# Normalised rows interleaved by eight tiles and fetched back in runs of 1 KB; weights of sorted rows loaded in five pieces

## The chip, the cores and the metric

The kernel runs on one core of a Trainium2 chip. The time is device microseconds of one execution. The engines are TensorE (PE, its weight loads PEld), VectorE (DVE), ScalarE (ACT), GpSimd (POOL) and SyncE (SP, which here only issues DMAs).

## What is computed

The input is `x` of shape (4, 32, 128, 128), float32: four images. Two layers follow each other.

```python
# layer 0, per image: xs is x cut in 2x2 patches, 128 channels x 4096 places
energy = einsum('bci,bcj->bij', q, q);  d = sqrt(diagonal(energy))
attn   = softmax(energy / (d_i * d_j))                # 4096 x 4096
x      = gamma * einsum('bcj,bij->bci', q, attn) + xs # back to an image
# layer 1, on tokens t of 128 numbers (4096 per image)
t = t + attn1(ln(t))   # linear attention, no softmax: ln(t) enters through K^T V, a gram of ln(t)
t = t + ffn(ln(t))     # 8 experts, each token takes the 2 with the largest router weights
```

## The kernel before

**Order of the work.** The four images go one after the other through layer 0 (`attend`), which is nearly all of TensorE's work: blocks of 512 x 512 energies (L671, out `pe`), their exponential on ScalarE (L674, `pr`), the product with the values (L559, `po`). The energies are symmetric, so a block is also used in its transposed place: VectorE turns it in groups of 32 x 32 (L482, tile `F`), one DMA stores it to DRAM (L592, `blocks<-F`), six fetch it back with the groups changed over (L607, `F<-blocks`; for diagonal blocks L616 and `F<-below`), and some fifty units of work later TensorE uses it (L495 and L515, `pg`).

The order of the instructions on PE, DVE, ACT and SP is written out when the program is built. Everything else is a generator of small steps, and a step is put in between the blocks of layer 0 when its turn comes. All of the DMAs named here, unless another queue is given, are issued by SP in that order, so that one that waits holds up those behind it.

**Layer 1 of images 0 to 2** runs while the next image is in layer 0. For each group `kc` of eight tiles (0 to 3; a tile has 128 tokens), `close_rows` divides the sums of layer 0, adds them to the tokens `T`, takes mean and variance of each token (L746 to L754 close them: `bs` holds six numbers per tile, and L748 reads one of the six for each of eight tiles) and normalises the rows on ScalarE: `normalise` (L758, L760), one activation per tile, into `xn[:, k, :D]`, a buffer of 32 tiles with 132 numbers each (128 and four for later). `gram_rows` (L778, L789) then adds up the products of each tile with itself on TensorE, in two groups of four tiles: the tile is both weights and moving operand. In the profile each float32 matmul has two records of matmul and two of weight load. Last, the eight tiles go to DRAM (L878, `rows<-xn`).

When all four groups are done, `matrix` (L887) makes one matrix of the gram and the weights. `attention_rows(u)`, again for eight tiles each, needs the rows transposed. `fetch_blocks` (L998) reads them back from DRAM with four DMAs (L1002, `blocks<-rows`), so that block (a, q) of 32 x 32 comes to place (q, a):

```python
blocks[ts(q, S)].rearrange("i k (a c) -> i k a c", c=S),          # S = 32
keep["rows", u][:, :, ts(q, S)].rearrange("(a i) k c -> i k a c", i=S),
```

VectorE then turns each 32 x 32 block with two transposes of 128 x 512 (L1014), the tokens are attended (L919), statistics taken again and the normalised tokens written to `xn` a second time.

**Sorted rows.** Half an image at a time (`sorted_experts(h)`), GpSimd scatters each token's row, with its expert's weight in column 128, to DRAM `xs[h]`, sorted by expert in 39 tiles (L1129). The second half is turned on TensorE. The first half (`turned_by_vector`, L1249) is turned on VectorE: `load_blocks` (L1211, L1215, four DMAs for four tiles) at every fourth step, `turn` (L1221) eight steps later, `four_products` (L1243) eleven steps later, and three steps further the result is multiplied by the tokens' weights (L1227, `factor`) and stored. `factor` is read ahead of the first `load_blocks`, for all 39 tiles in one DMA (L1252): elements of four bytes, 4992 of them.

**The last image** has no layer 0 beside its layer 1. Its rows never go through DRAM (`alone` is true; `transpose_rows` on TensorE does the turning), and its end is `last_parts`.

Of the kernel before, what the change touches and what calls it, by code (L numbers as in the profile page):

```python
# [12 lines left out]
F32 = mybir.dt.float32  # L13
BF16 = mybir.dt.bfloat16
U32 = mybir.dt.uint32
AF = mybir.ActivationFunctionType
# [6 lines left out]
def kernel(  # L23
# [43 lines left out]
    nc = tc.nc  # L67
    P = 128
# [8 lines left out]
    S = 32  # L77
    NH, KQ, D = wk.shape
# [10 lines left out]
    work = ctx.enter_context(tc.tile_pool(name="work", bufs=2))  # L89
    stat = ctx.enter_context(tc.tile_pool(name="stat", bufs=2))  # L90
    dram = ctx.enter_context(tc.tile_pool(name="dram", bufs=2, space=bass.MemoryType.DRAM))
# [626 lines left out]
    def layer1(b, st):  # L718
# [36 lines left out]
            if nm == "f":  # L755
                pinned(nc.gpsimd.tensor_scalar(nbo[:, rows], nb, 1.0, None, ALU.add))

        def normalise(rows, rs, nb):  # L758
            for k in rows:
                nc.scalar.activation(xn[:, k, :D], T[:, k, :], AF.Identity, scale=rs[:, k, :], bias=nb[:, k, :])  # L760

        def transpose_rows(g):
            pt, done = hold(f"ptx_{b}_{g}", partial(keep_rows, g))
# [14 lines left out]
        def gram_rows(rows):  # L778


            def add(p):
                if 0 in rows:
                    nc.vector.tensor_copy(gram, p[:, :D])
                else:
                    nc.vector.tensor_tensor(gram, gram, p[:, :D], ALU.add)

            p, done = hold(f"pgram_{b}_{rows[0]}", add)
            for k in rows:
                nc.tensor.matmul(p[:, :D], xn[:, k, :D], xn[:, k, :D], start=(k == rows[0]), stop=(k == rows[-1]))  # L789
            return done  # L790

        def close_rows(kc):


            def missing():
                return len(st["o"]) < 2 * kc + 2 or any(
                    st["got"][c] < NCH - c - (alone and c == NCH - 1) for c in (2 * kc, 2 * kc + 1)
                )

            late_rows = alone and kc >= 2  # L800
            last_rows = alone and kc == 3

            while "exps" not in st if last_rows else missing():
                yield from idle(1)
            while b > 0 and kc == 0 and not states[b - 1].get("sorted"):
                yield from idle(1)
            den, rd = (stat.tile([P, 2 * NJ], F32, tag=nm, name=f"{nm}_{b}_{kc}") for nm in ("den", "rd"))
            nc.vector.tensor_reduce(den, st["sums"][:, ts(kc, 2 * NJ), :], AX.X, ALU.add)
            nc.vector.reciprocal(rd, den)
            wide = work.tile([P, NJ, 2, 64], F32, tag="grp", name=f"rdx_{b}_{kc}", bufs=2)  # L810
            for s in range(2):
                one = rd[:, ts(s, NJ)][:, :, None]
                nc.vector.tensor_scalar(wide[:, :, s], one.to_broadcast([P, NJ, 64]), gam, None, ALU.mult)
            df = work.tile([P, 8, HW2, 2], F32, tag="df", name=f"df_{b}_{kc}", bufs=1)

            def divide(pb):
                for s in range(2):
                    own = slice(s * 64, s * 64 + 64)
                    o = st["o"][2 * kc + s]
                    for r2 in range(2):  # L820
                        rows = slice(r2 * 64, r2 * 64 + 64)
                        nc.vector.tensor_tensor(
                            df[own].rearrange("p (a k) (h t) r -> p r a (k h) t", a=4, h=2)[:, r2],
                            o[rows].rearrange("p (a j t) -> p a j t", a=4, t=S),
                            pb[own].rearrange("p (j a t) -> p a j t", a=4, t=S),
                            ALU.mult,
                        )

            yield
            if not last_rows:  # L830
                yield
                yield
            pb, done = hold(f"pbd_{b}_{kc}", divide)
            for j in range(NJ):
                nc.tensor.transpose(pb[:, ts(j, P)], wide[:, j].rearrange("p s c -> p (s c)"), ident)
            yield
            while missing():
                yield from idle(1)
            done()
            if not late_rows:  # L840
                yield
                yield
            tk = T[:, ts(kc, 8), :]
            nc.vector.tensor_tensor(tk, tk, df.rearrange("p k w r -> p k (w r)"), ALU.add)
            bs, stats = batch_stats("a", 8 * kc, 8)
            for j in range(8):
                stats[j]()
                if j == 3:
                    yield
                    yield  # L850
            close_stats("a", 8 * kc, 8, bs)
            yield from idle(1 if late_rows else 3)
            k = 8 * kc
            normalise(range(k, k + 4), rsa, nba)
            if late_rows:
                for j in range(k + 4, k + 8):
                    nc.vector.tensor_scalar(
                        xn[:, j, :D], T[:, j, :], rsa[:, j, :], nba[:, j, :], ALU.mult, ALU.add
                    )
            yield  # L860
            if last_rows:
                keep_running(36)
                done = gram_rows([k + j // 2 + 4 * (j % 2) for j in range(8)])
                yield
                done()
                return
            done = gram_rows(range(k, k + 4))
            yield
            done()
            if not late_rows:  # L870
                normalise(range(k + 4, k + 8), rsa, nba)
            yield
            done = gram_rows(range(k + 4, k + 8))
            yield
            done()
            if not alone:
                rows = dram.tile([P, 8, D], F32, tag="rows", name=f"rows_{b}_{kc}", bufs=4)
                nc.sync.dma_start(rows, xn[:, ts(kc, 8), :D])  # L878
                keep["rows", kc] = rows
            if alone and kc < 3:  # L880
                for g in (2 * kc, 2 * kc + 1):
                    yield
                    done = transpose_rows(g)
                    yield
                    done()
# [111 lines left out]

        def fetch_blocks(u):  # L998

            keep["blocks", u] = blocks = work.tile([P, 8, D], F32, tag="wide", name=f"blocks_{b}_{u}")  # L1000
            for q in range(4):
                nc.sync.dma_start(  # L1002
                    blocks[ts(q, S)].rearrange("i k (a c) -> i k a c", c=S),
                    keep["rows", u][:, :, ts(q, S)].rearrange("(a i) k c -> i k a c", i=S),
                )

        def attention_rows(u):
# [3 lines left out]
            yield  # L1011
            for g in (2 * u, 2 * u + 1):
                keep[g] = work.tile([P, CH], F32, tag="grp", name=f"xnT_{b}_{g}", bufs=2)
                nc.vector.transpose(keep[g], keep["blocks", u][:, ts(g % 2, 4), :].rearrange("p k d -> p (k d)"))  # L1014
                yield
            yield
            la = stat.tile([P, 8, 2 * E], F32, tag="la", name=f"la_{b}_{u}")
# [32 lines left out]
        def sorted_experts(h):  # L1050
# [156 lines left out]
            def read(inst):  # L1207
                wait_for(inst.ins, xs_made[h], "a tile holds tokens of any row")
                xs_read[h].append(inst.ins)

            def load_blocks(g, n):  # L1211
                rows = xs[h][4 * g * P : (4 * g + n) * P, :D].rearrange("(m i) w -> i m w", i=S)
                for q in range(4):
                    read(
                        nc.sync.dma_start(  # L1215
                            parts[g % 2][ts(q, S), : n * D].rearrange("i (m c) -> i m c", c=S), rows[:, :, ts(q, S)]
                        )
                    )
# [1 line left out]
            def turn(g, n):  # L1220
                nc.vector.transpose(parts[2 + g % 2][:, : n * D], parts[g % 2][:, : n * D])  # L1221

            def four_products(factor, g, n):

                def leave(p):
                    result = keep["results"].rearrange("p g j c -> p (g j) c")[:, ts(g % 2, 4)]
# [19 lines left out]
                    )  # L1246
                return done

            def turned_by_vector():  # L1249

                factor = stat.tile([P, NT, 1], F32, tag="factor", name=f"factor_{b}_{h}", bufs=1)
                read(nc.sync.dma_start(factor, xs[h].rearrange("(t p) w -> p t w", p=P)[:, :, D : D + 1]))  # L1252
                leaves = {}
                for at in range(4 * len(quads) + 10):
                    for first_at, act in (
                        (8, turn), (0, load_blocks), (11, partial(four_products, factor)), (13, lambda g, n: leaves.pop(g)()),
                    ):
                        if at >= first_at and (at - first_at) % 4 == 0 and (at - first_at) // 4 < len(quads):
                            g, n = quads[(at - first_at) // 4]
                            made = act(g, n)  # L1260
                            if first_at == 11:
                                leaves[g] = made
                    yield
# [380 lines left out]
```

## Time and profile before

| | |
|---|---|
| time before, median of 3 runs | 1620.63 us (1615.23 to 1624.31) |
| profiled execution, its own time | 1636.16 us |
| its span, granted TensorE clock | 1634.4 us, 0.994 |
| PE idle in the span (1634.4 - 1592.9) | 41.5 us |
| DMA queue of SP (q1) | 339776 packets, 308.23 MB, 63.6% of 16 engines |
| DMA packets in all | 374359, of them 159968 under 512 bytes |
| `normalise`, first time (L760, rsa) | 120 activations of 483 ns |
| `gram_rows` on PE (L789) | 256 records, mean 279 ns; 34.7 us busy |
| VectorE's turn of fetched rows (L1014) | 24 transposes, mean 692 ns |
| fetch of rows (L1002) | 48 DMAs of 128 KB |
| `factor` (L1252) | 3 DMAs of 19.5 KB |

A record of a matmul is longer than its share of TensorE's time, since matmuls are pipelined; the spacing of records in the chain tells the share. Idle time of an engine that is not the bottleneck costs nothing by itself. A wait for several things is put down to the one that came last. The trace also has a record of every DMA packet, with its size and the time that it took.

### The profile page before, as it was taken

The page shows a single profiled execution, that of the slowest core. Times are in us where ns is not written, and L with a number is a line of the kernel's source. Part 1 is how long each engine was busy: PE and PEld are TensorE (multiplying, and loading weights), DVE is VectorE, ACT ScalarE, POOL GpSimd, SP SyncE. Part 2 cuts the span into 40 slices and gives each one's busy share as a digit, 9 for nine tenths or more (in the row PEclk, how much of TensorE's full clock was granted, in tenths as well). Part 3 has the DMA queues.
Part 4 walks back from the last instruction along what each step waited for, and adds up shares of the span by engine and source line. Part 5 has one row for each costly group of instructions (what it writes and reads, how often), then busy time and mean ns, then how long its engine had stood idle before and what let it go on. Part 6 is the DMA issues. An engine that isn't in the chain of part 4 may idle for free.

```text
span 1634.4 us, 20871 instructions
## 1 busy us (share of the span) xinstructions
PE 1592.9 (97%) x5019; PEld 830.1 (51%) x5019; DVE 940.0 (58%) x2369; ACT 877.2 (54%) x2779; POOL 596.2 (36%) x567
## 2 busy tenths in 40 slices
PE   8999999999999999999999999999999999998987
PEld 5444544455554454555554445555555455554633
DVE  5443343477686454469478445449568454444786
ACT  4555445466475544556565544556556444544386
POOL 1000000010025541546555542446556641545166
PEclk9999999999999999999999999999999999999999
DMA  5554756676769698998999699998899898884001
GB/s 169 191 204 163 222 184 230 221 237 210 183 211 283 187 240 253 286 254 227 204 250 279 218 231 282 248 276 221 219 234 278 266 238 252 230 272 126 10 14 39
DMA packets 374359, 349.07 MB, mean 214 GB/s; under 512 B 159968, under 2 KB 300768, under 8 KB 359904
## 3 DMA queue, kind: packets, MB, share of 16 engines
q1 hardware_dynamic: 339776, 308.23, 63.6%
q0 software_dynamic: 26624, 25.58, 7.7%
q10 hardware_dynamic: 7840, 13.93, 2.9%
q8 instruction: 42, 0.69, 0.2%
q14 instruction: 77, 0.63, 0.1%
HBM read 170.57 MB, written 182.32 MB: 216 GB/s over the span
## 4 chain that ended last, share of the span: by engine, by line
PE 89%; DVE 3%; DMA 3%; SPq 2%; ACT 1%; issue 1%; another core or an unknown queue 1%; POOL 0%; ACTq 0%; DVEq 0%
PE po L559 26%; PE pe L671 26%; PE pg L495 22%; PE py L1434 3%; PE pg L515 2%; PE pys L1193 2%; PE pgram L789 2%; PE pat L919 1%; PE pys L1243 1%; SPq L607 1%; PE pys L1200 1%; DMA F<-blocks 1%; SPq L1215 1%; DMA ys<-results 0%
## 5 line engine op out<-in xcount | busy, mean ns | idle before, releaser
L674 ACT ACTIVATE pr<-pe 128x512 f32<-128x512 f32 (+1 forms) x576 | 322.5, 560 | 609.4 <-PE pe L671 509.8
L559 PE MATMUL po<-pr,qT 128*128 128x512 f32 (+3 forms) x1152 | 548.3, 558 | 0.2 <-ACT o L564 0.2
L671 PE MATMUL pe<-qn,qn 128*128 128x512 f32 x896 | 458.6, 594 | 3.5 <-ACT pr L674 2.1
L495 PE MATMUL pg<-F,qT 128*128 128x512 f32 x880 | 451.8, 595 | 8.1 <-DMA F<-blocks 5.4
L482 DVE STREAM_TRANSPOSE F<-pr 128x512 f32<-128x512 f32 x440 | 305.1, 699 | 149.2 <-ACT pr L674 128.5
L559 PEld LDWEIGHTS po<-pr,qT 128*128 128x128 f32 x1152 | 216.4, 190 | 240.4 <-issue 224.1
L500 ACT ACTIVATE junk<-F 128x512 bf16<-128x512 f32 x440 | 273.0, 620 | 5.7 <-DMA F<-blocks 4.9
L1308 POOL DMA_INDIRECT acc<-ys,place x128 | 203.2, 1587 | 192.3 <-ACT pr L674 120.3
L495 PEld LDWEIGHTS pg<-F,qT 128*128 128x128 f32 x880 | 166.8, 191 | 203.8 <-issue 179.0
L1129 POOL DMA_INDIRECT xs<-xn,place x192 | 187.1, 975 | 183.4 <-ACT pr L674 111.3
L671 PEld LDWEIGHTS pe<-qn,qn 128*128 128x128 f32 x896 | 157.7, 191 | 130.1 <-issue 119.6
L504 DVE TENSOR_TENSOR o<-o,pg 128x512 f32<-128x512 f32 x110 | 75.0, 682 | 210.9 <-PE pg L495 181.0
L164 POOL TENSOR_TENSOR norm<-ss,neg_half 128x8 f32<-128x8 f32 (+1 forms) x17 | 27.0, 1586 | 311.9 <-DVE ss L296 304.4
L674 ACT ACTIVATION_READ_ACCUMULATOR pr<-pe 128x1 f32 x576 | 111.9, 194 | 0.0
L1308 POOL DMA_INDIRECT yb<-ys,place x64 | 61.2, 956 | 88.0 <-ACT pr L674 47.3
L671 PE MATMUL pe<-qn 128*128 128x512 f32 (+3 forms) x256 | 90.2, 435 | 0.7 <-ACT qn L365 0.7
L500 ACT ACTIVATION_READ_ACCUMULATOR junk<-F 128x1 f32 x440 | 84.4, 192 | 0.0
L1175 DVE TENSOR_TENSOR results<-pys,xn 128x256 f32<-128x256 f32 (+1 forms) x60 | 25.0, 416 | 82.9 <-ACT xn L1169 54.5
L164 POOL TENSOR_TENSOR rsa<-dm_a,neg_half 128x8 f32<-128x8 f32 x16 | 28.4, 1775 | 113.0 <-DVE sv_a L752 112.9
L1434 PE MATMUL py<-ew_sb,xn 128*128 128x512 f32 x128 | 61.5, 622 | 5.1 <-ACT tmp L1390 3.9
L671 PEld LDWEIGHTS pe<-qn 128*128 128x128 f32 x256 | 45.1, 191 | 38.1 <-issue 33.7
L164 POOL TENSOR_TENSOR rsf<-dm_f,neg_half 128x8 f32<-128x8 f32 (+1 forms) x15 | 26.3, 1751 | 103.6 <-DVE sv_f L752 103.6
(226 smaller groups left out, 1506.1 us busy)
## 6 DMA issues: line engine op xcount, KB each, us to landing
blocks<-F SPq DMA_DIRECT2D x110, 1024.0 KB
F<-blocks SPq DMA_DIRECT2D x220, 192.0 KB
F<-blocks SPq DMA_DIRECT2D x220, 128.0 KB
F<-blocks SPq DMA_DIRECT2D x220, 64.0 KB
below<-F SPq DMA_DIRECT2D x31, 384.0 KB
T<-in_x_dram SPq DMA_DIRECT2D x64, 128.0 KB
out_dram<-acc SPq DMA_DIRECT2D x128, 64.0 KB
xa<-in_x_dram SPq DMA_DIRECT2D x62, 128.0 KB
```

Source lines behind the costliest of these rows:

```text
L164: pinned(nc.gpsimd.tensor_tensor(dst, src, neg_half.to_broadcast(list(src.shape)), ALU.pow))
L482: f()
L495: nc.tensor.matmul(pg.rearrange("p (a f) -> p a f", a=4), st["qT"][i][:, ib, :], G[:, :, ib], start=(ib == 0), stop=(ib == NJ - 1),)
L500: nc.scalar.activation(junk, G[:, :, ib], AF.Copy, accum_out=st["sums"][:, NJ * i + ib, jc : jc + 1])
L504: nc.vector.tensor_tensor(st["o"][jc], st["o"][jc], pg, ALU.add)
L515: nc.tensor.matmul(out[:, :, : ib * S], st["qT"][i][:, ib, :], rows, start=(ib == 3), stop=(ib == 1))
L559: nc.tensor.matmul(row["po"][:, lo:hi], qT[blk // NJ][:, blk % NJ, :], w, start=start, stop=(row["left"] == 0))
L671: nc.tensor.matmul(pe[:, c0:], qn[jc][:, ts(j, P)], qn[i][:, c0:], start=True, stop=True)
L674: nc.scalar.activation(pr[:, c0:], pe[:, c0:], AF.Exp, accum_out=sums[:, t, i : i + 1]).ins
L1129: inst = nc.gpsimd.indirect_dma_start(xs[h], offset(place[:, i, k : k + 1]), xn[:, k, :], None)
L1308: inst = nc.gpsimd.indirect_dma_start(to, None, ys, offset(place[:, i, k : k + 1]), compute_op=op)
L1434: nc.tensor.matmul(bank, xn[:, k, :D], ew_sb[:, 4 * h : 4 * h + 4, :], start=True, stop=True)
```

## The change

For images 0 to 2 the eight tiles of a group are written to `xn` so that the eight values of one feature lie next to each other: element (feature d, tile k) is at 8 d + k. One tile's features are then 32 bytes apart, for ScalarE's write and for both operands of the gram. The rows' copy in DRAM has the same order, so that a block of 32 features by eight tiles is one run of 1024 bytes, for the store and the fetch, and VectorE's turn reads elements that are 32 bytes apart. The last image keeps its rows.

The second edit moves the read of `factor` into `load_blocks`, which fetches eight tiles' weights ahead of every second group of four tiles: five DMAs for 39 tiles.

```diff
-        def normalise(rows, rs, nb):
+        def normalise(rows, rs, nb, to=None):
             for k in rows:
-                nc.scalar.activation(xn[:, k, :D], T[:, k, :], AF.Identity, scale=rs[:, k, :], bias=nb[:, k, :])
+                row = xn[:, k, :D] if to is None else side_by_side(to)[:, :, k - 8 * to]
+                nc.scalar.activation(row, T[:, k, :], AF.Identity, scale=rs[:, k, :], bias=nb[:, k, :])
+
+        def side_by_side(kc):
+
+            rows = xn[:, ts(kc, 8), :].rearrange("p k w -> p (k w)")[:, : 8 * D]
+            return rows.rearrange("p (d k) -> p d k", k=8)
...
-                nc.tensor.matmul(p[:, :D], xn[:, k, :D], xn[:, k, :D], start=(k == rows[0]), stop=(k == rows[-1]))
+                row = xn[:, k, :D] if alone else side_by_side(k // 8)[:, :, k % 8]
+                nc.tensor.matmul(p[:, :D], row, row, start=(k == rows[0]), stop=(k == rows[-1]))
...
-            normalise(range(k, k + 4), rsa, nba)
+            place_of = None if alone else kc
+            normalise(range(k, k + 4), rsa, nba, place_of)
...
-                normalise(range(k + 4, k + 8), rsa, nba)
+                normalise(range(k + 4, k + 8), rsa, nba, place_of)
...
-                rows = dram.tile([P, 8, D], F32, tag="rows", name=f"rows_{b}_{kc}", bufs=4)
-                nc.sync.dma_start(rows, xn[:, ts(kc, 8), :D])
+                rows = dram.tile([P, 4, 8 * S], F32, tag="rows", name=f"rows_{b}_{kc}", bufs=4)
+                nc.sync.dma_start(rows, side_by_side(kc).rearrange("p (c s) k -> p c (s k)", s=S))
...
-            keep["blocks", u] = blocks = work.tile([P, 8, D], F32, tag="wide", name=f"blocks_{b}_{u}")
+            keep["blocks", u] = blocks = work.tile([P, 4, S, 8], F32, tag="wide", name=f"blocks_{b}_{u}")
             for q in range(4):
                 nc.sync.dma_start(
-                    blocks[ts(q, S)].rearrange("i k (a c) -> i k a c", c=S),
-                    keep["rows", u][:, :, ts(q, S)].rearrange("(a i) k c -> i k a c", i=S),
+                    blocks[ts(q, S)].rearrange("i a s k -> i a (s k)"),
+                    keep["rows", u][:, q].rearrange("(a i) f -> i a f", i=S),
                 )
...
-                nc.vector.transpose(keep[g], keep["blocks", u][:, ts(g % 2, 4), :].rearrange("p k d -> p (k d)"))
+                nc.vector.transpose(
+                    keep[g].rearrange("p (k a s) -> p k a s", k=4, a=4),
+                    keep["blocks", u][:, :, :, ts(g % 2, 4)].rearrange("p a s k -> p k a s"),
+                )
...
             def load_blocks(g, n):
+                if g % 2 == 0:
+                    tiles = slice(4 * g, min(4 * g + 8, NT))
+                    read(
+                        nc.sync.dma_start(
+                            factor[:, tiles], xs[h].rearrange("(t p) w -> p t w", p=P)[:, tiles, D : D + 1]
+                        )
+                    )
...
+            if h == 0:
+                factor = stat.tile([P, NT, 1], F32, tag="factor", name=f"factor_{b}_{h}", bufs=1)
+
             def turned_by_vector():
 
-                factor = stat.tile([P, NT, 1], F32, tag="factor", name=f"factor_{b}_{h}", bufs=1)
-                read(nc.sync.dma_start(factor, xs[h].rearrange("(t p) w -> p t w", p=P)[:, :, D : D + 1]))
```

More of the change, by code (lines that the diff above doesn't have):

```diff
@@ L1221, in turn, with four_products @@
                 nc.vector.transpose(parts[2 + g % 2][:, : n * D], parts[g % 2][:, : n * D])
-            def four_products(factor, g, n):
+            def four_products(g, n):
                 def leave(p):
@@ L1255, in turned_by_vector @@
                     for first_at, act in (
-                        (8, turn), (0, load_blocks), (11, partial(four_products, factor)), (13, lambda g, n: leaves.pop(g)()),
+                        (8, turn), (0, load_blocks), (11, four_products), (13, lambda g, n: leaves.pop(g)()),
                     ):
```

## Prediction

> **What bounds the kernel now.** I read the page's busy row and chain first, then the windows of 40 us for the stages, then the waits of TensorE, then the chain and the SP queue around the two longest waits, then the lines by form for prices.
>
> ```profile
> PE 1592.9 (97%) x5019; PEld 830.1 (51%) x5019; DVE 940.0 (58%) x2369; ACT 877.2 (54%) x2779; POOL 596.2 (36%) x567
> PE 89%; DVE 3%; DMA 3%; SPq 2%; ACT 1%; issue 1%; another core or an unknown queue 1%; POOL 0%; ACTq 0%; DVEq 0%
> ```
>
> TensorE is busy for 97% of the span and is 89% of the chain; DMA and the SP queue together are 5%. So time can be won only where TensorE stands idle, and whatever TensorE has to do more is paid in full. The windows say where it is idle (time, length, then PE, PEld, DVE, ACT, POOL busy, clock, DMA share, GB/s):
>
> ```profile
> 800.00:840.00 40.00, 37.20 (x131) 20.86 (x130) 25.88 (x88) 22.21 (x70) 21.20 (x17) 1.00 0.96 218
> 840.00:880.00 40.00, 40.00 (x119) 20.12 (x118) 37.02 (x140) 25.72 (x81) 23.54 (x22) 1.00 0.91 273
> 1200.00:1240.00 40.00, 37.75 (x125) 20.22 (x124) 32.34 (x127) 26.71 (x79) 24.31 (x22) 1.00 0.93 252
> ```
>
> From 40 to 1480 us the idle of all windows adds to 15.2 us; the other 26 us are the first 40 us and the end after 1480, which the change doesn't touch (the last image keeps its rows as they were). Of the 15.2, windows 800 and 1200 hold 2.80 and 2.25. These are the stages in which images 1 and 2 fetch their normalised rows. The list of TensorE's waits names them, with everything else that is DMA or comes from the sorted rows:
>
> ```profile
> PE pg L495 <- DMA F<-blocks: 5.4, 3, 2.8
> PE pg L495 <- DVE F L482: 2.7, 3, 1.2
> PE pys L1243 <- DVE xn L1221: 0.6, 1, 0.6
> ```
>
> The SP queue before the wait of 2.8 us (start, time, line, count):
>
> ```profile
> 811.69 5.76 SPq L1002 DMA_DIRECT2D blocks<-rows  x4
> 817.56 0.71 SPq L592 DMA_DIRECT2D blocks<-F  x1
> 818.40 0.35 SPq L1032 DMA_DIRECT2D t<-T  x1
> 818.79 5.59 SPq L1002 DMA_DIRECT2D blocks<-rows  x4
> 829.42 2.68 SPq L607 DMA_DIRECT2D F<-blocks  x6
> ```
>
> The store of F at 817.56 sits between two fetches. Its way back at 829.42 waits for it to land, 11 us; in other places the same pair is 5 us apart (832.20 to 837.23, 963.63 to 968.29). The matmul at 835.01 waits for that way back. The chain names acc<-t as the releaser; a wait is put down to what came last, and L607 needs the store of F, so I take the store.
>
> **The change, part by part.** *Fetch (L1002).* 48 DMAs of 128 KB in pieces of 128 bytes are 49152 packets, 31% of the page's 159968 under 512 B; afterwards 48 x 128 = 6144 of 1 KB. In the trace's packet records one of 128 B takes 14.3 ns on the mean, 512 B 35.4, 2048 B 114.5; between the last two, 1 KB is some 62 ns. On 16 engines that is 44 us before and 24 after: 20 us of DMA time less, in stages where the DMA share is 0.8 to 1.1. SP's issue of four was 2.95 to 6.08 us; F<-blocks, with few packets, takes 2.67 for six, so 1.8 for four. The store of F at 817.56 goes out up to 4 us earlier and lands about 5 us after its issue: its way back starts near 823 at the latest, 6 us before 829.42. The wait of 2.79 goes. Image 2 has the same pattern (store at 1198.52, way back at 1211.37, 12.9 us), and its 2.25 goes. What is late next there: nothing, TensorE has no other wait from 825 to 840 or from 1205 to 1220. **-5.0 us.**
>
> *Store of rows (L878).* Same 12 DMAs, same bytes, but whole runs of 4 KB per partition where there were eight of 512 B. 12288 packets become 1536 or more; hidden, a little less load. Nothing.
>
> *Weights of sorted rows (L1252).* One DMA of 4992 four-byte elements becomes five of at most 1024, the same packets. Before, the first L1215 behind it stood 4.49 us in the SP queue (952.34), on the chain to the matmul that waited 0.63. After, 1024 elements stand ahead of it: about 0.9 us. **-0.6 us.** Each later piece puts about 0.9 us in front of every second load of four, and behind SP's L1215 wait the stores and ways back of F. VectorE's turn of a load comes eight half-steps later and already waits (DVE xn L1221 <- DMA xn<-xs: 37.3 us in 16 times), TensorE felt 0.6 of it; with 12 such pieces at most 12 x 0.9 = 11 us of VectorE waiting, below 1 us of it on TensorE by the same share. Four more DMAs for each of three halves, on SP alone; POOL's queue is not passed.
>
> *VectorE's turn (L1014).* 24 transposes of 692 ns now read with 32 bytes between elements. No transpose of before does; L315 reads at 8 bytes, 413 ns for 256 columns, on the line through 280 (128) and 564 (384). Lower end 0; upper end half speed, 512 x 1.07 = 0.55 us each, 13 us in all. Eight per image; VectorE is 37.0 of 40 us busy in window 840, so cover is thin there: 4.4 us for an image would leave 1 to 2 us on TensorE. *ScalarE (L760).* 96 activations of 483 ns write with 32 bytes between elements; 0 to 0.12 us each (half speed), 11.5 in all, on an engine that waits 510 us for L671. Covered: the grams' own wait for it is 0.5 us today. The rows of an octet now lie between each other: if waits are drawn by the range of bytes and not by the elements, the second four normalisations wait for the first gram (and with them the exponentials queued on ScalarE). That gram is issued half a step earlier and lasts 0.9 us; ScalarE waits for TensorE anyway, so 0, at most 12 x 0.9 = 11 us. I count 1 us for all of these.
>
> *Gram (L789).* This decides. Both operands, weights and moving rows, are now read with 32 bytes between elements, in 96 of 128 products, so 192 of these 256 records:
>
> ```profile
> L789 PE MATMUL pgram<-xn 128*128 128x128 f32 x256 | 34.7, 279 | 0.5 <-ACT xn L760 0.5
> L789 PEld LDWEIGHTS pgram<-xn 128*128 128x128 f32 x256 | 33.3, 191 | 11.8 <-issue 6.7 <-ACT xn L760 3.0 <-ACT pr L674 0.5
> ...
> L750 DVE TENSOR_TENSOR dm_a<-dm_a,sv_a 128x8 f32<-128x8 f32 x16 | 2.7, 167 | 0.5
> L748 DVE TENSOR_TENSOR dm_a<-bs_a 128x8 f32<-128x8 f32 x16 | 2.7, 166 | 0.0
> ```
>
> The chain, by time, has the products of four rows, two records each:
>
> ```profile
> 748.59 0.89 PE pgram L789 x8
> ```
>
> Eight records fill 0.89 us of the chain: 111 ns each, all on the path, no cover. No matmul of before reads elements apart. The nearest row is VectorE's: L748 reads two operands whose elements lie 24 bytes apart and takes 166 ns, L750 with close ones 167. Sixteen elements take 175 (L746), about 1 ns an element, so half speed would show as 8 ns; it doesn't. The Trainium skill speaks against the change: "SBUF — State Buffer", section "Door 1: The DMA port swizzle" (its note on cachelines), says that SBUF has lines of 16 bytes, that two hits per line are needed for full bandwidth, and that fp32 may be four elements apart for free; here it is eight, one hit per line. By the rule with a doubled time (my estimate; the page gives no factor) the grams cost 192 x 111 ns = 21.3 us; by the row, 0. I take 0, nearest to the row, but the row is another engine at about 1 ns an element where TensorE takes 0.83 (107 ns for 128 columns more, L559's 593 against 486), has eight elements, and has no weights read beside it. Both ends stay in the range.
>
> Sum against the profiled execution (1636.16 us, span 1634.4): -5.0 - 0.6 + 1 + 0.6 for the later pieces = -4.0. That execution is 15.5 us above the median; the waits were seen in it alone, and I apply the difference in us: 1620.6 - 4.0 = 1616.6, -0.25%. Changes within 0.5% (8.1 us) are about what a measurement of this kernel can't tell from none.
>
> **Rivals.** (1) *Likeliest, 0.50*: strided reads cost TensorE nothing or up to 15 ns a record (3 us): 1614 to 1620, within 0.5%. (2) *Slower: the gram reads at half speed.* Place: L789 in the stages 338 to 403, 748 to 785, 1122 to 1166; price 21.3 - 4.0 = +17, 1638. It turns to slower by over 0.5% at (8.1 + 4.0) / 192 = 63 ns a record, 1.6 times. For it: the rule, two strided streams at once, no cover. Against: VectorE's row. 0.32, with a tail over 1642 (0.06 of it) if weights and rows take turns at the port: another 21 us, 1659. (3) *In between*: a record at 1.04 ns an element, VectorE's pace: +27 ns, 5.1 us, or ScalarE and VectorE give back what the fetch gains: 1620 to 1628. For it: DVE 37.0 of 40. 0.12, a sixth of it over 0.5%. (4) *Hidden anyway*: the store of F is late for another reason (other traffic, the DMA share is 0.96), and the waits stay: 1620 to 1621, counted in case 3's lower half. (5) *Faster by over 0.5%*: 8.1 of the 15.2 us of idle would have to go, though 5.0 of it (windows 1280, 1400 and 1440, 2.12 + 1.52 + 1.39) lies where no rows are fetched: under 1612.5, 0.06.
>
> Faster 0.06, slower 0.32 + 0.02 = 0.34, same 0.60. The range takes the likeliest case and half speed, from 1612 to 1642, and leaves out some 0.06 on either side. The likeliest case's own range is 1614 to 1620.
>
> **What would show it.** Right: blocks<-rows issues in about 1.8 us for four, packets under 512 B fall by about 49000; no wait of pg L495 for F<-blocks above 0.5 us in the fetch stages; the first L1215 behind a factor load under 1.5 us; pgram still 0.89 us for eight, its LDWEIGHTS still 191. Wrong: pgram at 1.8 us for eight or LDWEIGHTS near 300 ns (rival 2); L1014 near 1.2 us or L760 near 0.6 with new TensorE waits for them (rival 3); the F<-blocks wait of 2 to 3 us still there (rival 4). A cost of the grams that shows only in the spacing of records, not in their length, would also make it wrong.

## The result, and the profile after

The changed kernel takes 1638.64 us (median of 6 runs, 1637.50 to 1642.01) against 1620.69 us before: ratio 1.0122, 95% interval 1.0106 to 1.0138. It is slower by 18 us between the medians (17 to 22 by the interval), where the likeliest case of the prediction was 4 us faster. The time lies within the range, at the place of rival 2 (1638).

The profiled executions can't be set against each other as wholes. That of before lay 15.5 us above its median: TensorE's granted clock fell to half in five spells (mean 0.994), where that of after has two (0.998), and some waits near the end are in it alone. So its span is only 2.4 us shorter than the one of after (1636.8). What follows is read line by line.

The page after, busy time and the chain by engine:

```profile
PE 1609.5 (98%) x5019; PEld 852.1 (52%) x5019; DVE 951.4 (58%) x2369; ACT 879.8 (54%) x2779; POOL 596.3 (36%) x567
...
PE 91%; DVE 3%; DMA 2%; SPq 2%; ACT 1%; issue 1%; POOL 0%; ACTq 0%; DVEq 0%
```

TensorE has as many instructions as before and is busy 16.6 us longer, its weight loads 22 us. The lines by form say where (the gram is L796 now, VectorE's turn L1022, ScalarE's normalisation L761):

```profile
L796 PE MATMUL pgram<-xn 128*128 128x128 f32 x256 | 58.3, 383 | 1.5 <-ACT xnT L781 0.9 <-ACT xn L761 0.6
L796 PEld LDWEIGHTS pgram<-xn 128*128 128x128 f32 x256 | 57.3, 296 | 10.0 <-issue 3.1 <-ACT xn L761 2.2 <-ACT xnT L781 1.2
L761 ACT ACTIVATE xn<-T,nba,rsa 128x128 f32<-128x128 f32 x120 | 51.7, 572 | 5.1 <-POOL nba L754 5.1
L1022 DVE STREAM_TRANSPOSE xnT<-blocks 128x512 f32<-128x512 f32 x24 | 25.8, 1085 | 9.8 <-PE pat L927 9.8
...
L750 DVE TENSOR_TENSOR dm_a<-dm_a,sv_a 128x8 f32<-128x8 f32 x16 | 2.7, 167 | 0.5
L748 DVE TENSOR_TENSOR dm_a<-bs_a 128x8 f32<-128x8 f32 x16 | 2.7, 166 | 0.0
```

The gram's matmuls are busy 58.3 us where they were 34.7, the turn went from 692 to 1085 ns, the activation from 483 to a mean of 572. The last two rows, on which the prediction had rested its choice, are as they were. In the chain, by time, the products of four rows:

```profile
339.50 1.89 PE pgram L796 x8
...
747.01 1.89 PE pgram L796 x8
...
1134.38 1.89 PE pgram L796 x8
```

That is 236 ns a record where it was 111. There are 24 such groups in images 0 to 2: 24 x (1.89 - 0.89) = 24.0 us, all on TensorE.

The windows that had 2.80 and 2.25 us of idle, and the thin cover of VectorE between them:

```profile
800.00:840.00 40.00, 40.00 (x138) 22.21 (x137) 23.34 (x60) 19.13 (x61) 20.89 (x15) 1.00 0.79 205
840.00:880.00 40.00, 40.00 (x126) 20.73 (x125) 36.22 (x136) 29.33 (x90) 25.57 (x22) 1.00 0.84 241
...
1200.00:1240.00 40.00, 39.91 (x148) 22.97 (x148) 29.88 (x90) 22.72 (x71) 22.38 (x18) 1.00 0.81 222
```

TensorE has no gap there any more (0.09 us is left), and the DMA share fell from 0.96 and 0.93 to 0.79 and 0.81. The packets under 512 bytes went from 159968 to 111008, 48960 fewer. Of TensorE's waits for the things named before, two are left:

```profile
PE pg L495 <- DMA F<-blocks: 2.8, 4, 0.9
...
PE pg L495 <- DVE F L482: 0.9, 1, 0.9
```

And the SP queue where the store of F stood between two fetches (the fetch is L1010):

```profile
822.60 2.40 SPq L1010 DMA_DIRECT2D blocks<-rows  x4
825.23 0.34 SPq L592 DMA_DIRECT2D blocks<-F  x1
831.17 0.34 SPq L1043 DMA_DIRECT2D t<-T  x1
831.57 2.23 SPq L1010 DMA_DIRECT2D blocks<-rows  x4
833.90 10.71 SPq L607 DMA_DIRECT2D F<-blocks  x6
```

The four DMAs of a fetch issue in 1.7 to 3.5 us where they took 3.0 to 6.1, and the way back of F begins 8.7 us after the store instead of 11.9. But only two of its six DMAs go then; the other four, in the same row, leave at 842.69:

```profile
842.69 1.92 SPq L607 DMA_DIRECT2D F<-blocks  x4
```

So the gaps that the change was built to close are closed, though not as the prediction had it (taken up below), and 24.0 us are lost elsewhere.

### The profile page after: what moved, and what is told of

The parts are those of the page before. It is cut to its first block, busy times and chain, and to the rows that moved or that the text cites. A ratio compares the mean times of both kernels' runs of the same rounds, so it can differ in the third digit from the quotient of the medians.

```text
span 1636.8 us, 20878 instructions
## 1 busy us (share of the span) xinstructions
PE 1609.5 (98%) x5019; PEld 852.1 (52%) x5019; DVE 951.4 (58%) x2369; ACT 879.8 (54%) x2779; POOL 596.3 (36%) x567
## 2 busy tenths in 40 slices
DMA packets 320792, 349.08 MB, mean 213 GB/s; under 512 B 111008, under 2 KB 245664, under 8 KB 306336
## 4 chain that ended last, share of the span: by engine, by line
PE 91%; DVE 3%; DMA 2%; SPq 2%; ACT 1%; issue 1%; POOL 0%; ACTq 0%; DVEq 0%
PE po L559 26%; PE pe L671 26%; PE pg L495 22%; PE pgram L796 3%; PE py L1453 3%; PE pg L515 2%; PE pat L927 2%; PE pys L1204 2%; PE pys L1261 1%; DMA F<-blocks 1%; SPq L1233 1%; PE pys L1211 1%; SPq L607 1%; PE pgv L912 0%; PE pm L918 0%
## 5 line engine op out<-in xcount | busy, mean ns | idle before, releaser
L495 PE MATMUL pg<-F,qT 128*128 128x512 f32 x880 | 450.0, 593 | 3.8 <-DMA F<-blocks 2.8
L495 PEld LDWEIGHTS pg<-F,qT 128*128 128x128 f32 x880 | 166.1, 190 | 199.1 <-issue 173.5
```

What stands on the lines that cost most here:

```text
L495: nc.tensor.matmul(pg.rearrange("p (a f) -> p a f", a=4), st["qT"][i][:, ib, :], G[:, :, ib], start=(ib == 0), stop=(ib == NJ - 1),)
```

## The experiments

The theory after this comparison (A): TensorE's reads of operands that lie apart are the whole loss, and the fetch still gains some 5 us. The rival (B): the slower activations and turns, or the moved traffic, make it. Each ratio below is against runs of the kernel before on the same chip, whose median is given as "beside it". Where the gram reads `T`, it adds up tokens before normalisation; the number and shapes of its products stay.

**gram_close.** The changed kernel without the strided gram.

```diff
-                row = xn[:, k, :D] if alone else side_by_side(k // 8)[:, :, k % 8]
+                row = xn[:, k, :D] if alone else T[:, k, :]
```

> The changed kernel, with one thing altered: for images 0 to 2 the gram reads the tokens before normalisation (contiguous rows of T) in place of the interleaved rows, so its output is not the reference's; ScalarE still writes interleaved rows, and store, fetch, turn and weights are those of the change. Theory A, TensorE's reads 32 bytes apart are the whole loss: eight records of pgram go back from 1.89 to 0.89 us, 24 x 1.0 = 24 us come back, 1638.6 - 24 = 1614.6, which is about 6 us below the kernel before (0.996). Theory B, the loss lies in ScalarE's and VectorE's slower instructions (0.11 us x 96, 0.39 us x 24) or in the traffic: the time stays above 1630 although pgram is 0.89.

Measured 1616.68 us, 0.9966 (0.9956 to 0.9976; 1622.13 beside it). The chain has the close price again, and the two windows of the fetch have no gap:

```profile
341.07 0.89 PE pgram L796 x8
...
800.00:840.00 40.00, 39.79 (x148) 22.95 (x147) 29.36 (x90) 22.19 (x71) 22.51 (x18) 1.00 0.83 221
...
1200.00:1240.00 40.00, 39.95 (x131) 21.28 (x130) 35.92 (x136) 28.06 (x84) 25.76 (x23) 1.00 0.81 230
```

Theory A, on both counts: the loss is gone, and what is left of the change is 5.5 us faster than before. ScalarE's and VectorE's instructions are as slow here as in the change (574 and 1084 ns), so they cost the end nothing that shows.

**gram_apart32.** The kernel before with the strided gram and nothing else.

```diff
-                nc.tensor.matmul(p[:, :D], xn[:, k, :D], xn[:, k, :D], ...)
+                apart = T[:, ts(k // 8, 8), :].rearrange("p k d -> p (k d)").rearrange("p (h d k) -> p h d k", d=D, k=8)
+                row = apart[:, k % 8 // 8, :, k % 8]          # images 0 to 2
+                nc.tensor.matmul(p[:, :D], row, row, ...)
```

> The kernel before, with one thing altered: for images 0 to 2 the gram reads tokens before normalisation, elements 32 bytes apart in T, for both operands; its output is not the reference's. Nothing else of the change is in it. Theory A: pgram at 1.89 us for eight records, 1620.6 + 24 = about 1644.6 (1.015). Theory B: below 1630.

Measured 1642.75 us, 1.0128 (1.0097 to 1.0159; 1622.13 beside it): +20.6 us by the medians, 16 to 26 by the interval, which holds A's +24 and is clear of B's 1630. The line by form has the price in both rows:

```profile
L794 PE MATMUL pgram<-T 128*128 128x128 f32 x192 | 49.0, 415 | 0.0
L794 PEld LDWEIGHTS pgram<-T 128*128 128x128 f32 x192 | 49.0, 332 | 6.2 <-issue 3.6 <-DVE sq L295 0.2
```

**weights_apart and moving_apart.** The same, with one operand apart and the other close.

```diff
+                nc.tensor.matmul(p[:, :D], apart, close, ...)  # weights_apart
+                nc.tensor.matmul(p[:, :D], close, apart, ...)  # moving_apart
```

> The kernel before, where the gram of images 0 to 2 takes its weights 32 bytes apart and its moving rows close together, both from tokens before normalisation (output not the reference's). With both apart a record took 236 ns where it takes 111 close. If weights and rows are read by the same port in turn, each has half of the cost: eight records of pgram about 1.4 us, +12 us, 1634. If they are read side by side and each is slow by itself: 1.89 us for eight (the slower sets the pace), +24 us, 1643. If only the moving rows cost: 0.89, 1622.

> The kernel before, where the gram of images 0 to 2 takes its moving rows 32 bytes apart and its weights close together, both from tokens before normalisation (output not the reference's). In turn at one port: about 1.4 us for eight records, +12 us, 1634. Side by side: 1.89 us, +24 us, 1643. If only the weights cost: 0.89, 1622.

Measured 1640.38 us, 1.0097 (1.0064 to 1.0130), and 1644.38 us, 1.0115 (1.0066 to 1.0164; 1624.27 beside both). In the chains, first of weights_apart and then of moving_apart:

```profile
339.40 1.77 PE pgram L794 x8
```

```profile
341.22 1.86 PE pgram L794 x8
```

Either operand alone has nearly the whole price (1.89 for both), and the two prices don't add: 0.89 + 0.88 + 0.97 would be 2.74. So the two slow reads overlap and the slower one sets the pace; taking turns, with half of the price each, is ruled out.

**gram_apart8.** As gram_apart32, with 8 bytes between elements.

```diff
+                row = T[:, ts(k // 8, 8), :].rearrange("p k d -> p (k d)").rearrange("p (h d k) -> p h d k", d=D, k=2)[:, k % 8 // 2, :, k % 2]
```

> The kernel before, where the gram of images 0 to 2 reads both operands 8 bytes apart (two elements in each 16 bytes), from tokens before normalisation (output not the reference's). At 16 and 32 bytes eight records took 1.85 and 1.89 us. If the cost comes with each new line of 16 bytes and two hits on a line hide it: 0.89 us, 1622. If any distance costs: above 1.3 us, 1632 or more.

Measured 1623.13 us, 0.9991 (0.9978 to 1.0005; 1624.27 beside it). The chain:

```profile
339.30 0.94 PE pgram L794 x8
```

0.05 us for eight records, 24 x 0.05 = 1.2 us in all. Two elements in 16 bytes hide the price almost wholly.

**four_apart.** The changed kernel with four tiles side by side, 16 bytes between elements.

```diff
-            return rows.rearrange("p (d k) -> p d k", k=8)
+            return rows.rearrange("p (h d k) -> p h d k", d=D, k=4)
```

> The changed kernel with four tiles side by side where it has eight: elements 16 bytes apart for ScalarE's write, the gram and VectorE's turn; the store in runs of 512 bytes (two DMAs a group), the fetch still in runs of 1 KB. If reads up to four fp32 apart are free[...]: pgram 0.89, L760 483 ns, the turn 692 ns, time 1614 to 1616 (0.997). If each new line costs (one hit per line here as with eight): pgram 1.89, as the change, 1638 (1.011). A value between says that the cost grows with the distance.

Measured 1640.27 us, 1.0119 (1.0091 to 1.0146; 1622.13 beside it), no better than eight. The chain, and the two other users by form:

```profile
340.64 1.85 PE pgram L796 x8
```

```profile
L761 ACT ACTIVATE xn<-T,nba,rsa 128x128 f32<-128x128 f32 x120 | 51.7, 573 | 5.2 <-POOL nba L754 5.2
...
L1023 DVE STREAM_TRANSPOSE xnT<-blocks 128x512 f32<-128x512 f32 x24 | 26.3, 1112 | 9.6 <-PE pat L928 9.6
```

The price jumps between 8 and 16 bytes (0.94, 1.85) and then stays (1.89 at 32). That fits the count of hits on a line of 16 bytes, two or one; a plain limit on the distance between 8 and 16 bytes would look the same, and no run here tells them apart. That fp32 may be four elements apart for free, which the Trainium skill ("SBUF — State Buffer", "Door 1: The DMA port swizzle") also says, does not hold here for any of the three engines: ScalarE's write and VectorE's turn are as slow at 16 bytes as at 32 (572 and 1085 ns).

**store_turned.** No interleaving; the order is changed by the store, in runs of 128 bytes, and the fetch keeps its runs of 1 KB.

```diff
+                for c in range(4):
+                    nc.sync.dma_start(rows[:, c], side_by_side(kc)[:, :, ts(c, S), 0])  # rows of one tile
```

> The changed kernel with rows of one tile kept whole in SBUF (no interleaving; ScalarE, gram and turn read and write contiguous runs of 32 or more), and the change of order made by the store: four DMAs a group in runs of 128 bytes, so that the fetch still has runs of 1 KB. Theory A: no compute cost, the fetch stages are relieved as in the change, the small packets move to the store where nobody waits: 1614 to 1617 (0.997). If the small packets do the same harm at the store: 1620, no difference.

Measured 1621.00 us, 0.9997 (0.9986 to 1.0009; 1622.13 beside it): no difference, though pgram is 0.89 and the fetch is relieved. The first of the two cases put down ahead of the run, that nobody waits at the store, was wrong. The windows show where the gain went:

```profile
720.00:760.00 40.00, 38.73 (x146) 22.78 (x145) 36.13 (x108) 25.79 (x84) 24.11 (x18) 1.00 0.78 184
760.00:800.00 40.00, 39.12 (x135) 21.33 (x134) 22.04 (x51) 23.83 (x76) 21.80 (x15) 1.00 0.92 234
...
1160.00:1200.00 40.00, 38.65 (x136) 21.62 (x135) 17.98 (x42) 19.37 (x62) 23.23 (x16) 1.00 0.97 235
```

3.5 us of idle in the stages of the store, none in gram_close, which has the same fetch (40.00 in all three). Two of the three waits there are pg L495 for F<-blocks (0.9 and 1.3 us), the third (1.3 us) is one for the gram's sum. So runs of 128 bytes cost at the store what the fetch gains. Whether they do it by their packets or by SP's time is not separated: SP takes 4.3 us or more for the four stores of a group in the last two of these windows, and gram_close's one store takes 0.4.

**factor_five.** The second edit alone.

> The kernel before with the second edit alone: the weights of the sorted rows in five loads. My sum has -0.6 us for the first and up to +0.6 for the later ones: no difference, 0.998 to 1.002; the wait of 4.49 us in the SP queue behind the first is gone. Rival: the later pieces hold up SP and VectorE and cost some us: 1.002 to 1.005, with new waits of pys L1243 and pg L495 between 570 and 640, 960 and 1040, and 1320 and 1400 us.

Measured 1623.76 us, 1.0007 (0.9988 to 1.0026; 1624.27 beside it): no difference. The longest load of four (L1215, here L1222) in its SP queue is 1.9 us instead of 4.49, and in the windows of the loads (560 to 640, 960 to 1040, 1320 to 1400) TensorE's idle is 2.9 us against 2.0 before. This run is also a second trace of the fetch stages without the first edit:

```profile
800.00:840.00 40.00, 37.66 (x138) 21.71 (x137) 26.75 (x89) 20.09 (x63) 21.12 (x17) 0.97 0.94 221
...
1200.00:1240.00 40.00, 38.23 (x136) 21.54 (x135) 32.12 (x128) 26.41 (x83) 22.30 (x20) 1.00 0.95 243
```

The gaps of 2.34 and 1.77 us are there again, so they weren't a chance of one execution.

**two_apart.** What the experiments point to: two tiles side by side, 8 bytes apart, stored in runs of 256 bytes, fetched in runs of 1 KB.

```diff
-            return rows.rearrange("p (d k) -> p d k", k=8)
+            return rows.rearrange("p (h d k) -> p h d k", d=D, k=2)
...
+                for n in range(4):
+                    nc.sync.dma_start(rows[:, :, n], side_by_side(kc)[:, n].rearrange("p (c s) k -> p c (s k)", s=S))
...
+                    nc.vector.transpose(keep[g][:, ts(n, CH // 2)]..., keep["blocks", u][:, :, 2 * (g % 2) + n]...)
```

> The changed kernel with two tiles side by side where it has eight: elements 8 bytes apart (two in each 16 bytes), which cost the gram 0.94 us for eight records against 0.89; the store in runs of 256 bytes (four DMAs a group), the fetch in runs of 1 KB, VectorE's turn in two halves. Theory A (each new line of 16 bytes costs, two hits hide it): pgram 0.94, L761 483 ns, the turns no slower than 413 ns for 256 columns; the fetch's gain of 5.5 us less part of what the small runs cost at the store (5 us with runs of 128 bytes): 0.997 to 0.999. Rival: ScalarE's write or VectorE's turn has its own threshold and is slower at 8 bytes, with waits of TensorE: 1.000 to 1.003.

Measured 1617.48 us, 0.9979 (0.9969 to 0.9988; 1620.85 beside it): faster than both kernels. pgram is 0.94, ScalarE and VectorE pay nothing or little:

```profile
L761 ACT ACTIVATE xn<-T,nba,rsa 128x128 f32<-128x128 f32 x120 | 49.2, 492 | 5.1 <-POOL nba L754 5.1
...
L1024 DVE STREAM_TRANSPOSE xnT<-blocks 128x256 f32<-128x256 f32 x48 | 17.9, 416 | 14.9 <-PE pat L928 14.7 <-DMA blocks<-rows 0.2
```

**woven_vector_2 and woven_pool_2.** The gram reads rows of one tile; another engine copies them into the order of the change.

```diff
+                woven = work.tile([P, 8 * D], F32, tag="wide", name=f"woven_{b}_{kc}")
+                nc.vector.tensor_copy(woven.rearrange("p (d k) -> p d k", k=8), xn[:, ts(kc, 8), :D].rearrange("p k d -> p d k"))
+                nc.sync.dma_start(rows, woven.rearrange("p (c f) -> p c f", c=4))
```

> The changed kernel, but ScalarE writes rows of one tile as before and the gram reads those; VectorE then copies the eight tiles into a separate tile with eight side by side (12 copies of 128x1024), and the store, issued right behind, reads that. VectorE's turn still reads 32 bytes apart (1084 ns). Theory A: TensorE pays nothing, pgram 0.89, and the fetch's gain stays if VectorE's copies (1.1 to 2.2 us each, 13 to 26 us) are covered: 0.9965 to 0.998, as fast as two tiles side by side or faster. Rival: VectorE is over 33 of 40 us busy in these stages, SP stands 2 us at each store, and TensorE waits for what comes late: 0.999 to 1.003.

> As woven_vector_2, with GpSimd making the 12 copies. Theory A: 0.9965 to 0.998, as GpSimd is busy 4 to 25 of 40 us there. Rival: SP stands for the length of each copy (some 3 us), and the powers of minus a half (rsa) and the gathers come later behind it, ScalarE and TensorE wait: 0.999 to 1.004.

Measured 1619.47 us, 0.9971 (0.9960 to 0.9983), with VectorE, and 1620.91 us, 0.9984 (0.9975 to 0.9993), with GpSimd (1623.12 beside both). Both beat the kernel before. VectorE's keeps most of the 5.5 us by its ratio and is not to be told from two_apart (the intervals overlap); GpSimd's copies take 2417 ns on the mean, and ScalarE waits 10.2 us for `nba` where it waited 5.1.

## Why the prediction was wrong

**The step that failed is the gram's.** It had 0 from VectorE's row (L748 against L750) and 21.3 us from the rule, and took 0, "nearest to the row". The runs have 24.0 us by the chain, +20.6 us by the time (gram_apart32). The row was true and is true after: VectorE reads eight elements 24 bytes apart in this instruction without loss. But it spoke for another engine and another instruction, and the prediction had named both as its weak points. Rival 2 had the place, the mechanism and, at 1638, the time, this in part because two misses offset each other (21.3 us where the chain has 24.0, -4.0 where gram_close has -5.5); a record takes 2.1 times as long where it assumed 2. Its first sign, pgram near 1.8 for eight, and its second, LDWEIGHTS near 300, are both there (1.89; 296 on the mean of all, 336 the median). Its tail, weights and rows taking turns, is ruled out by weights_apart and moving_apart. Had the sum taken the rule for this term, it would have been 1620.6 - 4.0 + 21.3 = 1637.9.

**The fetch** (-5.0): the size came out, the reading behind it did not, so it was in part luck. gram_close, which has everything but the gram's reads, is 5.5 us faster than before (3.9 to 7.1 by the interval), and the two named gaps are gone. But the prediction took the store of F for what the way back waited for, against the chain, and the trace of before shows that the chain was right. SP's wait for the store's semaphore, at 824.4, was over at once (17 ns; likewise in image 2, at 1206.1): the store had landed. Then SP stood for acc<-t, a DMA of ScalarE's queue:

```profile
L607 SPq EVENT_SEMAPHORE  x1: 17/17/17, 824.4 to 824.4; - x1
...
SPq L607 <- DMA acc<-t: 4.9, 1, 4.9
...
825.33 4.07 DMA acc<-t
```

So an earlier store could not bring the whole way back to 823. In gram_close two of its six DMAs do go at 822, and the other four stand for acc<-t all the same, 7.6 us long:

```profile
822.11 0.84 SPq L607 DMA_DIRECT2D F<-blocks  x2
...
827.82 0.33 ACTq L1315 DMA_DIRECT2D acc<-t  x1
...
830.60 1.71 SPq L607 DMA_DIRECT2D F<-blocks  x4
```

The gap closes by a narrow margin. SP goes on 2.8 us after the issue of acc<-t instead of 4.1 (3.6 in factor_five), with four DMAs left instead of six, so that the last leaves 4.1 us after it instead of 6.4 (5.8). TensorE then stands 0.2 us. How much of this is due to the smaller load of packets and how much to the order in the queue is not isolated. The sum also left out the clock: the mean granted clock is 0.9975 in the runs of gram_close and 0.9964 before, which is 1.8 of the 5.5 us (an estimate, 0.0011 x 1620 us); in factor_five the gap of 2.34 us is followed by half clock (0.50 from 838 to 840 us).

**The turn and ScalarE's write** (1 us together): the turn costs 0.39 us more, under the upper end of 0.55, ScalarE 0.11, next to its upper end of 0.12. Both were covered, even in window 840, where VectorE stays at 36 of 40 us: gram_close has them and loses nothing that shows. Waits drawn by byte range did not show: "PE pgram <- ACT xn" is 0.6 us, 0.5 before.

**The weights in five loads** (-0.6 and +0.6): no difference, as summed, but the interval (-1.9 to +4.2 us) could not show 0.6 us; the 4.49 us behind the first load went.

**The store** (nothing): nothing speaks against it for the change's long runs, which no run isolates. The opposite case, runs of 128 bytes, costs as much as the fetch gained (store_turned); the prediction didn't ask what the store's packets would do in the other direction.

Rival 3's ends that give back the gain are refuted by gram_close, rival 5 by the time. Of rival 4 the outcome (the gaps stay) is refuted by the windows, but its cause, other traffic that holds the way back, is what the trace shows. The chance of 0.34 for slower was too low: two strided streams with no cover on the busiest engine deserved more weight than a row of another engine with eight elements, and VectorE's own turn pays at 32 bytes, as the run now shows.

The sum with the measured terms: -5.5 (fetch and all the rest) + 24.0 = +18.5; measured +18.0 between the medians.

## What to carry to other kernels

A layout that makes DMA runs longer by putting elements apart in SBUF is paid by every engine that touches it: ask first whether the engine that sets the end is one of them, and leave fp32 elements at most 8 bytes apart, or let an engine with time to spare make the second layout. An operand pattern that the trace doesn't show on the engine in question has no price yet; a row of another engine is a weak bound, and where a stated rule speaks against it, the uncovered engine should be priced by the rule. Moving small DMA packets may only move the waits, where something urgent shares their queue. And a releaser that the chain names is set aside only when the trace shows that the other one came later.

## What was not expected of the hardware

TensorE's price is a step: 111 ns a record close, 118 at 8 bytes, 231 at 16, 236 at 32 (128 columns, fp32). VectorE's 32 x 32 transposes pay at 16 and 32 bytes (1112 and 1085 ns for 512 columns, 692 close), and not at 8 (416 for 256 columns). Its plain copy in woven_vector_2 puts eight rows 528 bytes apart into neighbouring elements, so that either the reads or the writes must jump with every element:

```profile
L887 DVE COPY woven<-xn 128x1024 f32<-128x1024 f32 x12 | 13.4, 1115 | 0.0
...
L449 DVE COPY wide<-norm 128x256 f32<-128x256 f32 x2 | 0.5, 289 | 0.6 <-POOL norm L164 0.6
L247 DVE COPY matx<-rw_sb 128x8 f32<-128x8 f32 x1 | 0.2, 159 | 0.0
```

Whether it pays is open. Beyond the 159 ns of a copy of eight elements (L247) it takes 0.94 ns an element, and the only other copy of some length within SBUF in this trace (L449, which repeats each number 64 times) takes 0.52. No run has the same copy with close elements.
